# A four-layer graph network on one core: source of the one-hot comparison, place of the first head's edge weights, order of background steps, and place of the degree computation

## The chip, the cores and the metric

The kernel runs on one core of one Trainium2 chip. The metric is device microseconds of one execution; the time of a version is the median of its runs. The core has TensorE (PE, matrix products into PSUM), VectorE (DVE), ScalarE (ACT), GpSimd (POOL) and SyncE (SP, which issues all the DMAs here). Each engine works through its own queue in order, and semaphores make engines wait for each other.

## The reference

There are 512 nodes with 768 features and 16384 edges from `src` to `dst`. Four layers each add a graph part and a mixing part to x, and then a feed-forward part. The parts that the change touches are these:

```python
# layer 0: 8-headed attention over the edges, then one head on its result; layer 1 is of the same kind
e = leaky_relu(alpha_s[src] + alpha_d[dst], 0.2)
e = exp(e - segment_max(e, dst)[dst])
alpha = e / (segment_sum(e, dst)[dst] + 1e-16)
out = segment_sum(h[src] * alpha[:, :, None], dst)
# layers 2 and 3: degrees with self loops
deg = segment_sum(ones, col)                 # col = dst and one loop for each node
norm = rsqrt(deg)[row] * rsqrt(deg)[col]
out = segment_sum((x @ W)[row] * norm[:, None], col) + b
```

## The kernel before

The edges are turned once into a dense table `cnt` (512 x 512, rows are destinations, cut in four tiles of 128): how often each pair of nodes occurs. All attention over edges is then dense: for each destination tile, a row of source scores (`row_of`, L323 on: four transposes on PE of a score column spread over 128 columns) is added to `off`, which holds -1e30 where `cnt` is zero; the maximum, leaky ReLU and exponential follow, and the product with `cnt`, row sums and division give weights. `turned` (L770) transposes them by source, and `aggregate` multiplies them with h on PE.

**Counting.** `edge_counts` (L668) takes 128 steps of 128 edges, in five groups. Each step makes two one-hots, one of 512 for the source (L702 on DVE, or L699 and L700 on ACT in every second or third step) and one of 256 for the destination (L703 on DVE: node numbers `near` against the edge's destination, then times 1 or 4096, so that one product counts two halves of the destinations). Two matmuls (L706) accumulate the count. `nodes` lies in SBUF as fp16; `near` is its first half as fp32 in PSUM. After each group, ACT, DVE and POOL split the two halves and add them to `cnt` (L712 to L721). At the end `off` is made (L723, DVE) and `cnt` is stored.

**Products.** A 768-wide product is done as one level of Strassen: `strassen` makes 14 calls of `product` (L503), each with three matmuls in fp32 (two passes each in the profile), and sums their PSUM results on DVE (L541 to L562) with copies on ACT (L525). In order, one half of the output rows needs products 1 and 2 (the loaded weights alone), 3 to 5 (weight differences), the other half 6 to 10 in the same way, and then 11 to 14. The weight differences come from POOL (`SplitB`, L436 to L439, three times four operations), the activation's sums from `SplitA` (L418 to L421). `strassen_add` (L602) does the same for products that are added to x or h2.

**Background steps.** `tick()` runs one step of the first generator in the list `background`; `product` calls it after its matmuls. `pinned` sets what a step issues behind the last instruction before it on each engine; counting is exempt (`loose`) and gets seven steps a tick. `delayed(n, ...)` lets n ticks go by. `drain()` runs what is left. Within these ties a planner decides each engine's order ahead of time, by the order of the program and its own estimate of when data is ready.

**Layer 0.** 24 steps of counting run alone, 16 more after the first norm, and the rest inside head 0's products. The loop over `i` (L911) computes head i's h and its scores (`heads`; `node_scores`, L783, eight operations on DVE that multiply h by a row and sum), while the weights of head i-1 are turned as steps (delayed 8). Then it aggregates head i-1, makes head i's weights (`edge_weights`, L735), and projects head i-1 (`project`, `L0_gnn_W2`).

**Layer 1.** `cnt` is loaded again; POOL makes a positive `off` (L1346), PE and ACT transpose `cnt` to `cntT` (L1350, L1351), and DVE sums the degrees (L1352). Then comes the product with `gat_w1`, with the steps of `second_norm` (a norm of the rows of xn on DVE and ACT, and their transposes). `rest` (the second half of the first norm's transposes and the activation's sums) is called after the first four products. `heads1` and `last_edges` are background steps in the products that follow.

**Layers 2 and 3.** `gcn` uses `dinv`, made from the degrees at L1692 to L1699.

Of the kernel before, what the change touches and what calls it, by code (L numbers as in the profile page):

```python
# [97 lines left out]
def kernel(ctx: ExitStack, tc: tile.TileContext, a: dict, out: bass.AP):  # L98
# [103 lines left out]
    def evacuate(dst, src):  # L202
# [3 lines left out]
        else:  # L206
            V.tensor_copy(dst, src)

    epsc = const.tile([P, 2], FP, name="epsc")
    G.memset(epsc[:, 0:1], 1e-5)  # L210
# [285 lines left out]
    def strassen(A, B, use, feature, then=None, extra=None, fresh=False):  # L496
# [5 lines left out]

        def product(bank, a, b, c, start, stop):  # L503
            for k in range(KC // 2):
                if feature:
                    l, r = b[:, k, ts(c, P)], a[:, k, :]
                else:
                    l, r = a[:, k, ts(c, P)], b[:, k, :]
                T.matmul(bank, l, r, start=start and k == 0, stop=stop and k == KC // 2 - 1,  # L509
                         skip_group_check=True)  # L510
            tick()

# [78 lines left out]
    def strassen_add(A, B, add, then=None):  # L591
# [4 lines left out]

        def product(m, name, l, r, start):
            b = banks[m]
            if start:
                b[name] = psum()[:, :HC]  # L600
            for k in range(KC // 2):
                T.matmul(b[name], l[:, k, ts(m, P)], r[:, k, :], start=start and k == 0,  # L602
                         stop=k == KC // 2 - 1, skip_group_check=True)
            tick()
            return b[name]
# [62 lines left out]
    def edge_counts(gp):  # L668
# [24 lines left out]
        for g in range(n_groups):  # L693
            js = range(EC * g // n_groups, EC * (g + 1) // n_groups)
            acc = [psum() for _ in range(2)]
            for j in js:
# [4 lines left out]
                else:  # L701
                    V.tensor_scalar(oh[:, :N], nodes, ef[:, 0, j : j + 1], None, op0=ALU.is_equal)  # L702
                V.tensor_scalar(oh[:, N:], near, ef[:, 1, j : j + 1], far[:, j : j + 1],  # L703
                                op0=ALU.is_equal, op1=ALU.mult)
# [17 lines left out]
        for t in range(NT):  # L722
            V.tensor_scalar(off[:, t, :], cnt[:, t, :], 0.0, -BIG, op0=ALU.is_equal, op1=ALU.mult)  # L723
        nc.sync.dma_start(cnt_dram, cnt)
# [9 lines left out]

    def edge_weights(src4, dst4, gp, cnt, off):  # L735

        srow = row_of(src4)
        w = gp.tile([P, NT, N], FP, tag="edge_w", name="edge_w", bufs=1)
        mx = tiny(NT, name="ga_mx")
        for t in range(NT):  # L740
            V.tensor_tensor_reduce(w[:, t, :], srow, off[:, t, :], 1.0, -3.0e38,  # L741
                                   ALU.add, ALU.max, mx[:, t : t + 1])
        V.tensor_add(mx, mx, dst4)
        nm = tiny(NT, name="ga_nm")
        V.scalar_tensor_tensor(nm, mx, 0.2, mx, op0=ALU.mult, op1=ALU.max)
        V.tensor_scalar(nm, nm, -1.0, None, op0=ALU.mult)
        den = tiny(NT, name="ga_den")
        for t in range(NT):
            wt = w[:, t, :]
            S.activation(wt, wt, AF.Identity, bias=dst4[:, t : t + 1])  # L750
            V.scalar_tensor_tensor(wt, wt, 0.2, wt, op0=ALU.mult, op1=ALU.max)  # L751
            S.activation(wt, wt, AF.Exp, bias=nm[:, t : t + 1])
            V.scalar_tensor_tensor(wt, wt, 1.0, cnt[:, t, :], op0=ALU.mult, op1=ALU.mult,  # L753
                                   accum_out=den[:, t : t + 1])
        V.tensor_scalar(den, den, 1e-16, None, op0=ALU.add)
        V.reciprocal(den, den)
        for t in range(NT):
            V.tensor_scalar(w[:, t, :], w[:, t, :], den[:, t : t + 1], None, op0=ALU.mult)
        return w

# [118 lines left out]
    with tc.tile_pool(name="gat0", bufs=2) as gp:  # L879
# [16 lines left out]
        def project(i, sums):  # L896
# [11 lines left out]
            flush()  # L908

        done = None  # L910
        for i in range(9):  # L911
            if done:
                g, hg, ew = done
                wT = gp.tile([P, NT, N], FP, tag="edge_wT", name="edge_wT", bufs=wt_bufs[0])
                if i < 8:
                    background.append(delayed(8, turned(ew, wT)))
                else:
# [8 lines left out]
            if i < 8:  # L926
                done = i, h, edge_weights(s4, d4, gp, cnt, off)
            else:
                ys, va = performer_values(norm)
            if i:  # L930
                project(g, sums)
        x = load_x()
        qT = last_gat(h2, "g0_as", "g0_ad", gp, cnt, off, lambda: performer_features(ys, 0))
# [403 lines left out]
    cntT = late.tile([P, NT, N], FP, name="cntT")  # L1337
    deg = late.tile([P, NT], FP, name="deg")
    dinv = late.tile([P, NT], FP, name="dinv")
    HW = 96  # L1340
    with tc.tile_pool(name="gat1", bufs=1) as gp:
        off = gp.tile([P, NT, N], BF, name="off")
        cnt = token_major("cnt")[:, :, :N]
        nc.sync.dma_start(cnt, cnt_dram)
        for t in range(NT):
            G.tensor_scalar(off[:, t, :], cnt[:, t, :], 0.0, BIG, op0=ALU.is_equal, op1=ALU.mult)  # L1346
        for s in range(NT):
            ps = psum()
            for t in range(NT):
                T.transpose(ps[:, ts(t, P)], cnt[:, t, ts(s, P)], ident)  # L1350
            S.copy(cntT[:, s, :], ps)  # L1351
        V.tensor_reduce(deg, cnt, AX.X, ALU.add)  # L1352

# [28 lines left out]

        background.append(second_norm())

# [305 lines left out]
    for s in range(NT):  # L1690
        V.tensor_add(cntT[:, s, ts(s, P)], cntT[:, s, ts(s, P)], ident)
    V.tensor_scalar(deg, deg, 1.0, None, op0=ALU.add)  # L1692
    S.activation(dinv, deg, AF.Sqrt)
    V.reciprocal(dinv, dinv)
    nw = tiny(NT, name="ln_nw")
    V.tensor_mul(nw, dinv, dinv)
    V.tensor_mul(nw, nw, deg)
    V.tensor_scalar(nw, nw, -0.5, 1.5, op0=ALU.mult, op1=ALU.add)
    V.tensor_mul(dinv, dinv, nw)  # L1699

# [328 lines left out]
```

## Time and profile before

| | |
|---|---|
| median of 3 runs | 3117.9 us (3116.71 to 3118.49) |
| the profiled execution: its own time | 3118.86 us |
| its span, first to last instruction | 3117.1 us |
| mean granted TensorE clock | 0.987 |
| TensorE busy | 3014.7 us, 97% |
| VectorE busy | 1508.9 us, 48% |
| GpSimd busy | 1451.9 us, 47% |
| ScalarE busy | 745.8 us, 24% |
| chain that ended last | PE 85%, DVE 10%, ACT 2%, POOL 2% |

How to read it: the span is what the profile records; the execution's own time is 1.8 us more, and the profiled execution lies 1.0 us above the median. Times in the views are counted from the span's start. Busy time of an engine is summed over the span; a busy TensorE is not always at its peak, since the ends of pipelined matmuls are modelled. In the timeline each line has the start, the length, the engine, the source line, the operation, its output and input names with their shapes, the number of merged instructions, and in brackets how long the engine had stood idle and who released it. A length there includes some 0.09 us in which the next instruction on DVE has begun; the pitch from start to start is what one costs.

### The profile page before, as it was taken

How to read it: one execution, taken by the hardware profiler on the slowest of the kernel's cores; microseconds unless marked ns; L12 is line 12 of the kernel's file. 1: busy time of each engine (PE TensorE's matmuls, PEld its weight loads, DVE VectorE, ACT ScalarE, POOL GpSimd, SP SyncE). 2: the span in 40 equal slices, each digit the busy share in tenths (PEclk: the TensorE clock that was granted, in tenths of full speed). 3: DMA queues.
4: the chain of work that ended last, by engine and by line, in shares of the span. 5: the costliest groups of instructions: out<-in, count | busy, mean ns of one | idle time of the engine just before them, and what ended most of it. 6: DMA issues, size and time to landing. Idle time of an engine off the chain costs nothing.

```text
span 3117.1 us, 31594 instructions
## 1 busy us (share of the span) xinstructions
PE 3014.7 (97%) x11757; PEld 2006.2 (64%) x11757; DVE 1508.9 (48%) x3420; ACT 745.8 (24%) x1426; POOL 1451.9 (47%) x1535
## 2 busy tenths in 40 slices
PE   7799999999999999999989999999999999999989
PEld 3355555555766776765675357877777776677755
DVE  8954545455356235446766535433333335462241
ACT  7332222242253112103532212200000002221111
POOL 2544444443425563565552343555555558255610
PEclk9899999999999999999999999999999999999999
DMA  3121212221302222421111512122212223122222
GB/s 115 54 71 71 71 71 71 71 92 59 98 6 97 91 92 70 126 105 56 62 66 62 152 66 95 68 91 91 86 71 88 92 91 122 48 100 68 101 85 61
DMA packets 92691, 253.63 MB, mean 81 GB/s; under 512 B 9889, under 2 KB 14881, under 8 KB 91514
## 3 DMA queue, kind: packets, MB, share of 16 engines
q1 hardware_dynamic: 92538, 251.61, 23.3%
q8 instruction: 93, 1.52, 0.2%
q14 instruction: 60, 0.49, 0.1%
HBM read 244.23 MB, written 7.36 MB: 81 GB/s over the span
## 4 chain that ended last, share of the span: by engine, by line
PE 85%; DVE 10%; ACT 2%; POOL 2%; issue 1%; DMA 0%; SPq 0%; POOLq 0%; DVEq 0%; ACTq 0%
PE ps L509 41%; PE ps L602 23%; PE ps L888 5%; PE ps L306 4%; PE ps L1077 1%; DVE oh L703 1%; PE ps L1064 1%; PE ps L296 1%; PE ps L272 1%; PE ps L1910 1%; DVE edge_w L751 1%; PE ps L1565 1%; DVE edge_w L741 1%; DVE edge_w L753 1%; PE ps L1923 1%
## 5 line engine op out<-in xcount | busy, mean ns | idle before, releaser
L436 POOL TENSOR_TENSOR tw<-w 128x384 f32<-128x384 f32 x246 | 252.0, 1035 | 948.5 <-DMA w<-in_L_gnn_W 336.8
L509 PE MATMUL ps<-sx,w 128*128 128x256 f32 x1188 | 316.7, 380 | 3.6 <-DVE sx L418 2.8
L509 PE MATMUL ps<-sx,tw 128*128 128x256 f32 x1188 | 292.0, 382 | 4.2 <-DVE room L1434 3.2
L602 PE MATMUL ps<-w,sx 128*128 128x384 f32 x720 | 256.8, 486 | 4.4 <-DVE sx L418 3.1
L438 POOL TENSOR_TENSOR tw<-w 128x384 f32<-128x384 f32 x246 | 255.6, 1047 | 9.3
L439 POOL TENSOR_TENSOR tw<-w,tw 128x384 f32<-128x384 f32 x246 | 254.2, 1042 | 10.1
L437 POOL TENSOR_TENSOR w<-w 128x384 f32<-128x384 f32 x246 | 252.7, 1037 | 8.6
L509 PEld LDWEIGHTS ps<-sx,tw 128*128 128x128 f32 x1188 | 220.2, 190 | 47.7 <-DVE st_u L549 8.2
L602 PE MATMUL ps<-tw,sx 128*128 128x384 f32 x720 | 250.4, 487 | 0.0
L509 PEld LDWEIGHTS ps<-sx,w 128*128 128x128 f32 x1188 | 224.8, 190 | 39.3 <-PE ps L509 2.3
L525 ACT COPY st_p<-ps 128x256 f32<-128x256 f32 (+1 forms) x127 | 49.9, 394 | 719.7 <-PE ps L509 680.9
L549 DVE TENSOR_TENSOR st_u<-st_p,ps 128x256 f32<-128x256 f32 (+1 forms) x127 | 57.2, 450 | 337.3 <-PE ps L509 337.1
L602 PEld LDWEIGHTS ps<-tw,sx 128*128 128x128 f32 x720 | 136.1, 190 | 95.1 <-DVE x L1794 1.2
L602 PEld LDWEIGHTS ps<-w,sx 128*128 128x128 f32 x720 | 136.4, 190 | 94.5 <-POOL tw L439 4.3
L652 DVE TENSOR_TENSOR x<-x,ps 128x384 f32<-128x384 f32 x216 | 115.2, 552 | 165.7 <-PE ps L602 164.3
L509 PE MATMUL ps<-xfT,w 128*128 128x256 f32 x720 | 176.8, 380 | 0.2
L509 PE MATMUL ps<-w,sx 128*128 128x384 f32 x456 | 169.1, 490 | 2.4 <-DVE up_r L719 1.7
L888 PE MATMUL ps<-edge_wT,h 128*128 128x512 f32 x384 | 166.1, 592 | 0.0
L509 PE MATMUL ps<-tw,sx 128*128 128x384 f32 x456 | 162.2, 490 | 2.2 <-DVE st_u L549 2.1
L552 DVE TENSOR_TENSOR st_u<-st_p,ps 128x256 f32<-128x256 f32 (+1 forms) x127 | 57.2, 450 | 206.0 <-PE ps L509 206.0
L509 PEld LDWEIGHTS ps<-xfT,w 128*128 128x128 f32 x720 | 135.9, 190 | 24.1 <-issue 1.3
L602 PE MATMUL ps<-w,hid 128*128 128x384 f32 x432 | 142.9, 488 | 0.0
(482 smaller groups left out, 5111.0 us busy)
## 6 DMA issues: line engine op xcount, KB each, us to landing
w<-in_L_gnn_W SPq DMA_DIRECT2D x60, 768.0 KB, 6.4
w<-in_L_mix_fc_w SPq DMA_DIRECT2D x48, 768.0 KB, 6.4
row<-in_rows SPq DMA_DIRECT2D x39, 384.0 KB, 4.4
w<-in_L_mix_qkv_w SPq DMA_DIRECT2D x18, 768.0 KB, 5.2
w<-in_L_ffn_w SPq DMA_DIRECT2D x18, 768.0 KB, 7.1
w<-in_L_ffn_routed_gate SPq DMA_DIRECT2D x18, 768.0 KB, 5.9
w<-in_L_ffn_routed_up SPq DMA_DIRECT2D x18, 768.0 KB, 6.8
w<-in_L_ffn_routed_down SPq DMA_DIRECT2D x18, 768.0 KB, 5.7
```

The lines of the kernel that those rows point to most:

```text
L306: T.matmul(ps, parts[k][:, ts(t, P)], w_of(k)[:, ts(c, HC)], start=k == 0, stop=k == n - 1)
L436: G.tensor_sub(tt[:, 0, k], b22[:, k], b12[:, k])
L437: G.tensor_sub(b12[:, k], b12[:, k], b11[:, k])
L438: G.tensor_sub(tt[:, 1, k], b22[:, k], b12[:, k])
L439: G.tensor_sub(tt[:, 2, k], b21[:, k], tt[:, 1, k])
L509: T.matmul(bank, l, r, start=start and k == 0, stop=stop and k == KC // 2 - 1, skip_group_check=True)
L525: S.copy(b["p1"], b["x"])
L549: V.tensor_add(b["u2"], b["p1r"], b["y"])
L552: V.tensor_add(u3, b["p1r"], b["y"])
L602: T.matmul(b[name], l[:, k, ts(m, P)], r[:, k, :], start=start and k == 0, stop=k == KC // 2 - 1, skip_group_check=True)
L652: V.tensor_add(x[:, t, ts(j, HC)], x[:, t, ts(j, HC)], ps)
L888: T.matmul(ps, h[:, s, ts(f, P)], wT[:, s, :], start=s == 0, stop=s == NT - 1)
```

## The change

1. `edge_counts`: from step 32 (the 33rd) on, L703 compares `nodes[:, :HT]` (fp16, SBUF) in place of `near` (fp32, PSUM).
2. `off` in layer 0 is made by four ACT operations, Relu(1e30 - 1e30 cnt), in place of four on DVE; it is positive now, and L741 subtracts it.
3. `edge_weights` becomes a generator `weighing` that stops after `row_of`, after the maxima, and after each second tile. Head 0 doesn't make its weights after its own products: in head 1 they are background steps after five idle ticks, and the turning follows with no idle ticks. Other heads call it in one piece as before.
4. Both `product` functions call `tick()` ahead of their matmuls.
5. `deg` and `dinv` are computed from `cnt` in layer 0, written after head 1's projection (`degrees`), with a constant tile for `dinv`; the code at L1352 and L1692 to L1699 goes.
6. Layer 1: `second_norm` gets three idle ticks; the transposes of `cnt` and `off` (now on ACT) become the steps of `by_sources` behind it.

```diff
+    bigc = const.tile([P, 1], FP, name="bigc")
+    G.memset(bigc, BIG)
...
         def product(bank, a, b, c, start, stop):
+            tick()
             for k in range(KC // 2):
...
-            tick()
...
         def product(m, name, l, r, start):
+            tick()
             b = banks[m]
...
-            tick()
             return b[name]
...
-                V.tensor_scalar(oh[:, N:], near, ef[:, 1, j : j + 1], far[:, j : j + 1],
+                V.tensor_scalar(oh[:, N:], near if j < 32 else nodes[:, :HT], ef[:, 1, j : j + 1], far[:, j : j + 1],
                                 op0=ALU.is_equal, op1=ALU.mult)
...
         for t in range(NT):
-            V.tensor_scalar(off[:, t, :], cnt[:, t, :], 0.0, -BIG, op0=ALU.is_equal, op1=ALU.mult)
+            S.activation(off[:, t, :], cnt[:, t, :], AF.Relu, bias=bigc, scale=-BIG)
...
-    def edge_weights(src4, dst4, gp, cnt, off):
+    def weighing(w, src4, dst4, cnt, off):
 
         srow = row_of(src4)
-        w = gp.tile([P, NT, N], FP, tag="edge_w", name="edge_w", bufs=1)
+        yield
         mx = tiny(NT, name="ga_mx")
         for t in range(NT):
             V.tensor_tensor_reduce(w[:, t, :], srow, off[:, t, :], 1.0, -3.0e38,
-                                   ALU.add, ALU.max, mx[:, t : t + 1])
+                                   ALU.subtract, ALU.max, mx[:, t : t + 1])
...
+        yield
         den = tiny(NT, name="ga_den")
...
+            if t % 2:
+                yield
...
+    def edge_weights(src4, dst4, gp, cnt, off):
+        w = weight_tile(gp)
+        for _ in weighing(w, src4, dst4, cnt, off):
+            pass
         return w
...
+        dinv = const.tile([P, NT], FP, name="dinv")
+
+        def degrees():
+            deg = tiny(NT, name="deg")
+            V.tensor_reduce(deg, cnt, AX.X, ALU.add)
+            V.tensor_scalar(deg, deg, 1.0, None, op0=ALU.add)
+            S.activation(dinv, deg, AF.Sqrt)
+            V.reciprocal(dinv, dinv)
...
                 if i < 8:
-                    background.append(delayed(8, turned(ew, wT)))
+                    if i == 1:
+                        background.append(delayed(5, weighing(ew, s4, d4, cnt, off)))
+                    background.append(delayed(0 if i == 1 else 8, turned(ew, wT)))
...
-                done = i, h, edge_weights(s4, d4, gp, cnt, off)
+                done = i, h, edge_weights(s4, d4, gp, cnt, off) if i else weight_tile(gp)
...
+            if i == 2:
+                degrees()
...
-        for t in range(NT):
-            G.tensor_scalar(off[:, t, :], cnt[:, t, :], 0.0, BIG, op0=ALU.is_equal, op1=ALU.mult)
-        for s in range(NT):
-            ps = psum()
-            for t in range(NT):
-                T.transpose(ps[:, ts(t, P)], cnt[:, t, ts(s, P)], ident)
-            S.copy(cntT[:, s, :], ps)
-        V.tensor_reduce(deg, cnt, AX.X, ALU.add)
+
+        def by_sources():
+            for s in range(NT):
+                ps = psum()
+                for t in range(NT):
+                    T.transpose(ps[:, ts(t, P)], cnt[:, t, ts(s, P)], ident)
+                S.copy(cntT[:, s, :], ps)
+                S.activation(off[:, s, :], cnt[:, s, :], AF.Relu, bias=bigc, scale=-BIG)
+                yield
...
-        background.append(second_norm())
+        background.append(delayed(3, second_norm()))
+        background.append(by_sources())
...
-    V.tensor_scalar(deg, deg, 1.0, None, op0=ALU.add)
-    S.activation(dinv, deg, AF.Sqrt)
-    V.reciprocal(dinv, dinv)
```

## The prediction

> **What bounds the kernel now.** The page comes first: engine totals.
>
> ```profile
> PE 3014.7 (97%) x11757; PEld 2006.2 (64%) x11757; DVE 1508.9 (48%) x3420; ACT 745.8 (24%) x1426; POOL 1451.9 (47%) x1535
> ```
>
> TensorE (PE) is the bound of nearly the whole span; only stretches where it stands idle or runs below its pace can give time back. The change touches three. I cut the span there with the view of busy time by stretch.
>
> ```profile
> core 0: us, PE busy (x) PEld busy (x) DVE busy (x) ACT busy (x) POOL busy (x), PEclk, DMA share, GB/s
> 39.50:119.90 80.40, 72.16 (x283) 32.34 (x281) 77.39 (x184) 44.10 (x74) 15.50 (x12) 1.00 0.00 1
> 119.90:172.10 52.20, 36.48 (x106) 19.57 (x106) 46.85 (x70) 13.62 (x25) 38.14 (x28) 0.80 0.26 82
> 172.10:250.99 78.89, 77.69 (x238) 42.66 (x237) 37.50 (x78) 23.92 (x42) 34.94 (x36) 1.00 0.20 70
> ...
> 1416.27:1440.00 23.73, 16.83 (x63) 10.32 (x62) 15.59 (x34) 9.32 (x20) 16.70 (x15) 0.86 0.10 42
> ```
>
> Row 1 is edge counting from about step 33 on beside head 0's products: VectorE (DVE) is full. Row 2 runs from head 0's last product to head 0's aggregation. Row 3, one later head, shows PE full: nothing to win there. Row 4 is the start of layer 1. What PE does at full clock, from matmul pitches in the timeline (0.215 us for L706, 0.323 for a 384-wide L509 pass, 0.108 for a transpose): row 1 has 193 L706 + 78 L509 + 12 transposes = 41.5 + 25.2 + 1.3 = 68.0, so 12.4 us are lost; row 2 has 84 L509 + 20 transposes = 29.3, so 22.9 are lost. Next, PE's waits in the first 200 us (total us, times, longest), and its timeline (start, us; in brackets idle before and who ended it).
>
> ```profile
> PE ps L706 <- DVE oh L703: 14.9, 7, 10.0
> PE ps L327 <- DVE st_u L783: 12.4, 4, 10.2
> ```
> ```profile
> 130.10 0.48 PE L327 MATMUL ps<-ident,ga_sc 128*128 128x128 f32 x1 [10.18 <-DVE st_u L783]
> ...
> 158.51 0.33 PE L774 MATMUL ps<-ident,edge_w 128*128 128x128 f32 x1 [0.35 <-DVE edge_w L758]
> ...
> 1425.90 5.97 PE L509 MATMUL ps<-w,xnT 128*128 128x384 f32 x12 [5.59 <-ACT st_p L525]
> ```
>
> 10.0 of the 14.9 us precede the first one-hot and stay. The 10.18 us is row_of's first transpose at the head of PE's queue, with head 1's products, whose first two need only loaded weights, behind it.
>
> **Node numbers from SBUF (96 steps).**
>
> ```profile
> 52.66 1.35 DVE L702 TENSOR_SCALAR oh<-nodes,ef 128x512 bf16<-128x512 f16 x1
> ...
> 54.98 0.34 DVE L702 TENSOR_SCALAR oh<-nodes,ef 128x512 bf16<-128x512 f16 x1
> 55.24 0.99 DVE L703 TENSOR_SCALAR oh<-ps,ef,far 128x256 bf16<-128x256 f32 x2
> ```
>
> L703 has a pitch of 0.45 us. No row has two pointers on fp16 in SBUF. Nearest is L702: 512 columns, one pointer, pitch 0.26. Half the columns save about 0.07; the second pointer adds at most 0.13 (two-pointer L280 is 0.457 where the plain copy L207 of the same PSUM shape is 0.33). That gives 0.19 to 0.27; the other bound is no gain, 0.47 (256 columns at the 1.04 ns of the 768-wide L420, plus pointers). I take 0.27, nearest the row: 96 x 0.18 = 17 us off DVE, whose 77.4 fall to 60, below PE's 68.0. PE becomes the bound. Against this speaks the Trainium skill, SBUF — State Buffer, "SBUF: two separate sides": a VectorE operation in a two-port mode and a GpSimd operation lock each other out for a whole instruction. The 1.35 us row, beside a POOL add, shows it for L702. Taken for every new L703 beside the 16 adds of 1.3 us, the rule would cost up to 16 us and eat the 17. But only as many waits can occur as adds, and L702 and L717 already suffer one or so per group (1.0, 0.4, 1.1, 0.5 us): I count no more than 4 us extra, inside DVE's new 8 us of slack. Of the 12.4 lost I leave 3.4 for group ends (PE's pauses of 1.4, 0.8, 0.9 us around L719): **gain 9.0**, bounds -2 and 12.4. Head 0 then ends at T = 119.9 - 9.0 = 110.9.
>
> **Head 0's weights as steps in head 1, `off` on ACT.** The four L723 (1.2, 1.2, 0.4, 1.2 us) leave DVE; four ACT operations of about 0.6 us (like L700's 0.63) come, beside an ACT 26% busy in row 2: free, or 2.4 us if it were the last. Subtracting a positive `off` in L741 is the same operation (0.61), and bigc's memset (0.1 us) falls in POOL's idle time before 11.5 us. srow's transposes stand before product 6, so PE no longer waits 10 us. What is late next is POOL, which makes head 1's weight differences while locked with node_scores:
>
> ```profile
> 127.10 2.12 POOL L436 TENSOR_TENSOR tw<-w 128x384 f32<-128x384 f32 x2
> ...
> 142.53 1.98 POOL L437 TENSOR_TENSOR w<-w 128x384 f32<-128x384 f32 x2
> ...
> 159.39 1.05 POOL L439 TENSOR_TENSOR tw<-w,tw 128x384 f32<-128x384 f32 x1
> ```
>
> It starts 7.2 us after counting's last matmul; with ticks ahead, counting ends two products (3.9 us) before T, so at T+3.4. Product 3 needs the L437 that ended 17.4 us after the start: T+20.8. Products 1, 2, 6, 7 fill PE's first 7.8 us; 3 to 5 end at T+26.6. Scores (3 us of leftovers + 8 x 1.67) are done by T+17. The weights' maxima are pinned behind product 5's sum, T+26.6. Before, the weights took 141.65 to 160.65 less 1.5 of other work = 17.5 us, locked with POOL; head 1's own took 193.18 to 202.98 plus scaling = 11.3, unlocked. POOL is busy to T+36.7: 10.1 us cover 58% of the work, 42% of 11.3 = 4.8 follow, plus 1.5 for chunk 1's sums: T+43. The other seven products end at T+40.2. With 1.2 for the first transposes and copy, aggregation starts at T+44.2, against 52.2 before: **gain 8.0**, bounds -1.7 (first rival) and 21.7 (PE's 29.3 plus 1.2).
>
> **Steps ahead of products elsewhere.** Each step moves one product (1.3 to 1.9 us) earlier; spacing, hence the chain behind each, stays. turned, the routers, heads1 and last_edges have row 3's kind of slack: 0, bounds -3 and +3. SP's row loads in those steps move with them, ahead of weight loads issued tens of us before use.
>
> **Degrees.** The planner hoists work whose data is ready:
>
> ```profile
> 2.94 0.17 DVE L1240 TENSOR_SCALAR qb<-cols 128x6 f32<-128x6 f32 x1
> ```
>
> So the reduction may land right after the counts, where DVE waits from T+17 to T+26.6: 2.3 us plus tiny operations (up to 0.9 each beside POOL), and a Sqrt that can cost two 1.28 us table loads. Hidden in that gap; uncovered, up to 5.5 + 2.6. I take **-0.5**. The four dinv operations at 1775.4 to 1778.8 leave no PE wait: 0.
>
> **Layer 1.**
>
> ```profile
> 1417.06 2.29 DVE L1352 TENSOR_REDUCE deg<-cnt 128x4 f32<-128x2048 f32 x1 [0.19 <-issue]
> ...
> 1420.19 2.13 DVE L1692 TENSOR_SCALAR deg<-deg 128x4 f32<-128x4 f32 x1
> ```
> ```profile
> 1424.46 1.03 ACT L252 ACTIVATE xn<-xn,ln_nb,ln_rs 128x768 f32<-128x768 f32 x1 [1.23 <-DVE ln_nb L251]
> 1425.39 0.84 ACT L525 COPY st_p<-ps 128x384 f32<-128x384 f32 x2
> ```
>
> The copies that products 3 and 4 of PE's queue need sit on ACT behind the second norm, which sits behind deg on DVE. With deg gone, norm steps three products later and cntT after them, the copies run at about 1418.3. PE: four products to 1424.0, rest's transposes 1.3, their copies 1.1, early's two 3.9, so first sums at 1430.3 against 1439.97. Of these 9.7, 1.3 (y's transposes) and 1.7 (cntT's) are moved, not saved: **gain 6.5**, bounds 2 and 8. `off`'s 7.9 us leave POOL, idle there anyway; ACT gains 4 x 0.6 beside the last products. cnt holds its buffer some 25 us longer; xnT's comes free first, so I cost that at 0 (up to 2).
>
> **Sum.** 9.0 + 8.0 - 0.5 + 6.5 = 23.0. Span 3117.1 - 23.0 = 3094.1; that execution took 3118.9, 1.8 outside the span: 3095.9; the median 3117.9 is 1.0 below it: **3095**.
>
> **Rivals.**
> - Queue order in head 1 (0.14): the transposes of ew stand ahead of products 11 to 14. For: at 158.51 the planner put them so, and PE waited. Against: by unlocked times it will find the weights late. Then aggregation is at T+43 + 9.6 + 1.3 = T+54: head 1 gives -1.7, sum 13.3: 3105.
> - L703 keeps its pace (0.09): first gain 0, sum 14: 3104. That is the change not doing what it says.
> - POOL releases early (0.09): products 3 on start ten us sooner, aggregation near T+34, counting at its floor: 9 + 3 + 18 + 6.5 - 0.5 = 36: 3082.
> - Slower (0.08): the same wedge, with degrees' 5.5 and table loads' 2.6 us in front of the weights, and PE's clock halved after the wait (in 130 to 140 the granted clock was 0.50, a pass 0.69 us). Products 11 to 14 then take 15.5; aggregation is at weights + 18.5. With counting's 9.0 and layer 1's 6.5 kept, the total turns slower from weights at T+49 (49 + 18.5 against 52.2 + 15.5); at T+51 it gives 3120, at T+55 3124.
> - Forecast (0.60): 3087 to 3103.
>
> A measurement of this kernel tells about 0.2% (6.2 us) from no change. Faster is forecast, queue order, pace and early POOL: 0.92. Of the slower case 0.06 lies within 0.2%, 0.02 beyond. The range 3084 to 3109 takes in the rivals at 3104 and 3105; it leaves out the early-POOL case and the slower one, 0.17.
>
> **What would show it.** L703 after step 32 at a pitch near 0.27; row 1's work ending near 111 us with DVE no longer full; L327 without a 10 us wait; the first L888 near 155; a lone wait of products 3 for POOL's L437; no st_p wait near 1420 and the first sums product about 9 us after the fourth. Wrong: L774 early in PE's queue with a long wait, L703 at 0.45, or deg between the weights.

## The result and the profile after

The changed kernel takes 3098.89 us (median of 4 runs, 3097.94 to 3099.33) where the kernel before takes 3117.31 (4 runs, 3113.12 to 3118.49): a ratio of 0.9943, 95% interval 0.9926 to 0.996, so faster by 0.57%. The forecast was 3095, range 3084 to 3109. The profiled execution took 3099.04 us, its span is 3097.2, 19.9 less than before; the forecast for the span was 23.0 less.

The engine totals of the changed kernel, and its busy time by stretch (its two rows answer to rows 1 and 2 of the prediction's view; in brackets the count of instructions):

```profile
PE 3005.4 (97%) x11757; PEld 2006.2 (65%) x11757; DVE 1482.7 (48%) x3416; ACT 749.7 (24%) x1434; POOL 1436.3 (46%) x1532
```
```profile
core 0: us, PE busy (x) PEld busy (x) DVE busy (x) ACT busy (x) POOL busy (x), PEclk, DMA share, GB/s
40.80:111.20 70.40, 67.33 (x269) 34.10 (x268) 62.87 (x178) 43.34 (x74) 18.20 (x14) 0.98 0.00 1
111.20:156.30 45.10, 34.31 (x105) 19.45 (x104) 37.42 (x68) 14.80 (x26) 31.52 (x27) 0.89 0.31 107
```

Counting beside head 0 takes 70.4 us in place of 80.4, and DVE (62.9 busy) is no longer full; PE is the fuller engine, as forecast. The timeline of DVE there shows the one-hots' pitch, 0.25 to 0.26 us for L705 (L703 before) and for L704 (L702 before):

```profile
85.01 0.34 DVE L704 TENSOR_SCALAR oh<-nodes,ef 128x512 bf16<-128x512 f16 x1
85.28 0.33 DVE L705 TENSOR_SCALAR oh<-nodes,ef,far 128x256 bf16<-128x256 f16 x1
85.53 0.34 DVE L704 TENSOR_SCALAR oh<-nodes,ef 128x512 bf16<-128x512 f16 x1
```

PE's waits in the first 200 us (total, times, longest): the wait for node_scores ahead of row_of (12.4 us) is gone, and a wait for GpSimd's weight differences (L439; L437 before) of 10.1 us has come. PE's timeline in head 1 shows where:

```profile
PE ps L708 <- DVE oh L705: 13.9, 4, 11.3
PE ps L512 <- POOL w L439: 10.1, 2, 6.7
```
```profile
128.41 1.65 PE L512 MATMUL ps<-w,sx 128*128 128x384 f32 x2 [6.72 <-POOL w L439]
129.86 3.85 PE L512 MATMUL ps<-tw,sx 128*128 128x384 f32 x6
...
136.39 0.60 PE L329 MATMUL ps<-ident,ga_sc 128*128 128x128 f32 x4
...
156.30 1.88 PE L901 MATMUL ps<-edge_wT,h 128*128 128x512 f32 x4
```

The six matmuls at 129.86 take 3.85 us where six at 134.35 take 2.20: after the wait PE runs at a lower clock (0.50 from 126.6 to 133.4 us, 0.89 over the stretch). row_of's transposes then start without a wait, and the aggregation starts at 156.30, against 171.94.

**The path cut in four.** A is first one-hot matmul to aggregation (counting and head 1), C is from the start of layer 0's last product to the first kv,qT product of layer 1's linear attention, D is all that follows. What lies between A and C is 1236.9 to 1237.6 us in every kernel here, and the first one-hot matmul comes at 10.0 us before, 11.3 after and 10.3 to 11.2 in the others: A, C and D don't contain that accident. Times in us.

| kernel | median | ratio to before (95%) | span | A | C | D |
|---|---|---|---|---|---|---|
| before | 3117.3 | | 3117.1 | 161.9 | 203.4 | 1504.4 |
| changed | 3098.9 | 0.9943 (0.9926 to 0.996) | 3097.2 | 145.0 | 199.2 | 1504.7 |
| e1 one-hot from PSUM | 3112.2 | 0.9972 (0.9961 to 0.9983) | 3109.8 | 158.3 | 199.2 | 1504.8 |
| e2 weights whole | 3105.9 | 0.9951 (0.9938 to 0.9965) | 3106.2 | 151.8 | 201.1 | 1505.2 |
| e3 steps behind | 3092.4 | 0.9908 (0.9895 to 0.9922) | 3091.5 | 148.0 | 194.5 | 1500.5 |
| e4 degrees late | 3101.7 | 0.9937 (0.9924 to 0.9949) | 3101.6 | 144.2 | 201.1 | 1508.1 |
| e9 ahead in heads 0, 1 only | 3089.5 | 0.9915 (0.9902 to 0.9929) | 3090.8 | 144.1 | 194.8 | 1504.1 |
| e10 one tick later | 3101.5 | 0.9951 (0.9938 to 0.9965) | 3100.8 | 144.5 | 203.8 | 1504.9 |
| e11 e9, split free | 3084.8 | 0.9897 (0.9884 to 0.9911) | 3083.8 | 139.3 | 195.9 | 1500.5 |
| e12 e9, nodes in all steps | 3096.5 | 0.9933 (0.9921 to 0.9945) | 3094.5 | 148.7 | 194.7 | 1503.6 |
| e13 step before split | 3099.8 | 0.9949 (0.9937 to 0.9962) | 3098.0 | 144.5 | 201.1 | 1504.9 |
| e14 e11, layer 1 as before | 3091.2 | 0.9925 (0.9913 to 0.9938) | 3089.0 | 138.9 | 198.7 | 1503.7 |
| e15 e3, split free | 3086.3 | 0.9906 (0.9892 to 0.992) | 3087.2 | 142.2 | 195.8 | 1500.5 |
| e16 e11, norm at once | 3088.7 | 0.9913 (0.9899 to 0.9927) | 3086.7 | 139.5 | 195.7 | 1503.5 |

e1 to e4, e9 to e12 and e13 to e16 each shared one chip with runs of before, at 3121.05, 3116.51 and 3116.24 us. A ratio's interval is about 4 us to each side, the changed kernel's 5. The four kernels with equal code in A (changed, e9, e10, e13) have 144.1 to 145.0 us there, so less than 0.9 decides nothing in A. In C and D equal code agrees only to the 2 to 3 us of the granted clock (last section). There a second split helps: the time in which PE stood idle (the stretch less PE's busy time), and the busy time lost to a lower clock (half of what PE was busy while the traces' clock records say 0.50). The first is read from these rows, C of before, of the changed kernel and of e3:

```profile
1409.35:1612.73 203.38, 182.52 (x920) 134.99 (x919) 141.50 (x347) 90.10 (x169) 109.25 (x95) 0.95 0.15 58
1393.27:1592.45 199.18, 179.71 (x920) 132.08 (x919) 135.93 (x344) 93.02 (x172) 101.26 (x91) 0.98 0.16 57
1396.48:1590.97 194.49, 180.60 (x920) 133.62 (x918) 132.15 (x344) 92.57 (x172) 100.64 (x91) 0.96 0.17 60
```

PE is idle for 20.9, 19.5 and 13.9 us of C, and loses 7.6, 3.2 and 5.5 us to the clock. In A the two stand in for each other: in the four kernels with equal code 17.8 to 21.5 us are idle and 7.2 to 3.0 lost to the clock, and the sum is 24.5 to 25.3.

### The profile page after: what moved, and what is told of

Read it like the earlier page. It is cut to its first block, busy times and chain, and to the rows that moved or that the text cites. A ratio compares the mean times of both kernels' runs of the same rounds, so it can differ in the third digit from the quotient of the medians.

```text
span 3097.2 us, 31606 instructions
## 1 busy us (share of the span) xinstructions
PE 3005.4 (97%) x11757; PEld 2006.2 (65%) x11757; DVE 1482.7 (48%) x3416; ACT 749.7 (24%) x1434; POOL 1436.3 (46%) x1532
## 3 DMA queue, kind: packets, MB, share of 16 engines
q8 instruction: 93, 1.52, 0.2%
## 4 chain that ended last, share of the span: by engine, by line
PE 86%; DVE 8%; POOL 2%; ACT 2%; issue 1%; DMA 0%; SPq 0%; POOLq 0%; ACTq 0%
PE ps L512 43%; PE ps L605 23%; PE ps L901 5%; PE ps L308 4%; PE ps L1109 1%; PE ps L1096 1%; PE ps L298 1%; PE ps L274 1%; PE ps L1934 1%; PE ps L1597 1%; POOL room L1455 1%; DVE edge_w L754 1%; DVE edge_w L743 1%; PE ps L1947 1%; PE ps L1324 1%
## 5 line engine op out<-in xcount | busy, mean ns | idle before, releaser
L439 POOL TENSOR_TENSOR w<-w 128x384 f32<-128x384 f32 x246 | 252.7, 1036 | 8.8
L441 POOL TENSOR_TENSOR tw<-w,tw 128x384 f32<-128x384 f32 x246 | 251.7, 1030 | 10.3
L551 DVE TENSOR_TENSOR st_u<-st_p,ps 128x256 f32<-128x256 f32 (+1 forms) x127 | 57.1, 450 | 346.7 <-PE ps L512 346.6
L512 PE MATMUL ps<-w,sx 128*128 128x384 f32 x456 | 170.3, 494 | 11.9 <-POOL w L439 10.1
L554 DVE TENSOR_TENSOR st_u<-st_p,ps 128x256 f32<-128x256 f32 (+1 forms) x127 | 57.1, 449 | 200.8 <-PE ps L512 200.8
```

Source lines behind the costliest of these rows:

```text
L439: G.tensor_sub(b12[:, k], b12[:, k], b11[:, k])
L441: G.tensor_sub(tt[:, 2, k], b21[:, k], tt[:, 1, k])
L551: V.tensor_add(b["u2"], b["p1r"], b["y"])
L554: V.tensor_add(u3, b["p1r"], b["y"])
```

## The experiments

**e1, e2, e3, e4: one part of the change undone each.** e1 takes the node numbers of L705 from PSUM again:

```diff
-V.tensor_scalar(oh[:, N:], near if j < 32 else nodes[:, :HT], ...
+V.tensor_scalar(oh[:, N:], near, ...
```

> The changed kernel, but L705 compares the PSUM copy of the node numbers in all 128 steps. Theory A (VectorE's pace of 0.45 us a step bounded the counting): head 0's last product ends near 119 us again instead of 111.2, everything after it as in the changed kernel, so 3107 to 3108 us. Theory B (the 8.7 us come from counting standing ahead of the products): head 0 ends at 111 to 113, 3099 to 3101 us.

Head 0's last product ends at 118.9, so theory A holds: counting was bound by VectorE. A grows by 13.3 us and the span by 12.6, more than either theory allowed. Counted from the first one-hot, 8.4 of the 13.3 lie ahead of head 0's end; the other 4.9 lie in head 1, where PE now waits 5.0 us for a copy of ScalarE (st_p). By the ratios the whole is 0.29%, 9 us.

e2 makes head 0's weights in one piece again, after head 0's products:

```diff
-if i == 1:
-    background.append(delayed(5, weighing(ew, s4, d4, cnt, off)))
-background.append(delayed(0 if i == 1 else 8, turned(ew, wT)))
+background.append(delayed(8, turned(ew, wT)))
...
-done = i, h, edge_weights(s4, d4, gp, cnt, off) if i else weight_tile(gp)
+done = i, h, edge_weights(s4, d4, gp, cnt, off)
```

> The changed kernel, but head 0's edge weights are made in one piece ahead of head 1's products, as before, and turned after eight idle ticks. Theory A (the first transposes at the head of TensorE's queue cost the wait): TensorE waits 8 us or more for scores, aggregation starts about 7 us later after head 0's end (52 against 45.1), 3106 us. Theory B (GpSimd's differences of head 1's weights bound the stretch in either order): aggregation at 45 to 47 us after head 0's end, 3099 to 3101 us.

A grows by 6.8 us, 6.2 of them idle time of PE. The aggregation starts 52.2 us after head 0's end, as theory A had it, and the wait for node_scores is back in PE's waits of the first 200 us:

```profile
PE ps L329 <- DVE st_u L796: 9.8, 4, 6.2
```

C differs by 1.9 us, of which 1.7 lie where the code is the same and the granted clock was 0.96 in place of 1.00. By the ratios the whole is 2.5 us with an interval wider than that, so the size is read from A.

e3 puts `tick()` behind the matmuls again in both `product` functions:

```diff
         def product(bank, a, b, c, start, stop):
-            tick()
             for k in range(KC // 2):
...
+            tick()
...
```

> The changed kernel, but each step stands behind its product again. Theory A (the order only sets when counting ends against head 0's last product, and with it when GpSimd may start on head 1's weights): counting ends with head 0, GpSimd starts some 4 us later, aggregation about 4 us later, 3102 to 3104 us. Theory B (the order is free): 3098 to 3100 us. In layer 1 both expect less than 1.5 us of difference.

This is faster than the change: 0.9908 against 0.9943, 5.7 us by the spans. A is 3.0 us longer, near theory A's 4, but C is 4.7 shorter and D 4.2, where both theories had allowed less than 1.5. In C it is PE's waits that fell (13.9 us of idle time against 19.5), not the clock. In D, 2.4 us are `last_edges` (31.2 us from its first product to L1597's in place of 33.6) and 1.1 a stretch whose granted clock was higher. The prediction had put all of this at 0.

e4 computes the degrees in layer 1 again, the reduction after the load of `cnt` and the rest ahead of layer 2:

```diff
-            if i == 2:
-                degrees()
...
         nc.sync.dma_start(cnt, cnt_dram)
+        V.tensor_reduce(deg, cnt, AX.X, ALU.add)
...
```

> The changed kernel, but the degrees are summed in layer 1 from the reloaded counts, and the rest of their code stands before the graph convolutions, as before. Theory A (with the second norm three products later, the reduction on VectorE blocks nothing that TensorE waits for; in layer 0 the degree operations stood in front of the weights' maxima for about 0.8 us): 3098 to 3100 us. Theory B (the degree operations were what made TensorE wait 5.6 us at the start of layer 1): a wait of 4 to 5 us for the st_p copies returns, 3102 to 3104 us.

By the ratios there is no difference. A is 0.8 us shorter, but that lies ahead of the last one-hot matmul, where the code is the same: from its end to the aggregation it is 48.8 us both with the degrees and without. C is 1.9 longer and D 3.4, mostly by the clock (2.2 and 2.6 us more lost to it); PE's idle time in C is 19.2 us against 19.5, and the wait for st_p did not return, so theory B fell, and theory A's time was missed by less than the clock took. What the degrees did in the changed kernel shows in DVE's timeline: the reduction ran right after counting, and their small operations, 3.0 us in all, stood ahead of L554 and the weights' maxima (L743). L554's product ended near 136.5, so L554 was some 0.7 us late, but nothing of this reached the aggregation:

```profile
113.86 2.29 DVE L928 TENSOR_REDUCE deg<-cnt 128x4 f32<-128x2048 f32 x1 [1.77 <-POOL cnt L723]
...
136.49 0.84 DVE L936 TENSOR_TENSOR dinv<-dinv,ln_nw 128x4 f32<-128x4 f32 x1
137.25 0.54 DVE L554 TENSOR_TENSOR st_u<-st_p,ps 128x384 f32<-128x384 f32 x1
...
138.30 0.68 DVE L743 CUSTOM_DVE_ANT_0 edge_w<-ps,off 128x512 f32<-128x512 f32 x1
```

**Where steps ahead of products cost.** PE's waits for the exponentials in heads1 (L1464 for L1457) between 1440 and 1600 us are 5.4 us in before, 11.3 in the changed kernel, 5.6 in e3. The longest in the changed kernel, 5.36 us, in the timeline of all engines:

```profile
1547.31 0.99 POOL L441 TENSOR_TENSOR tw<-w,tw 128x384 f32<-128x384 f32 x1
1548.26 2.49 POOL L1455 TENSOR_TENSOR room<-room 128x512 f32<-128x512 f32 x2
1549.55 0.72 ACT L1457 ACTIVATE room<-room,ed_b 128x512 f32<-128x512 f32 x1 [6.31 <-POOL room L1455]
...
1550.33 0.90 PE L1464 MATMUL ps<-ident,room 128*128 128x128 f32 x3 [5.36 <-ACT room L1457]
```

The L441 is the last of twelve SplitB operations (1536.16 to 1548.30) that GpSimd worked through ahead of the two subtractions the step needed. In e3 the planner put the same subtractions between the SplitB operations, and PE waited 1.17 us here and 1.52 for the second one, 2.7 us less than the changed kernel:

```profile
1545.10 1.25 POOL L1455 TENSOR_TENSOR room<-room 128x512 f32<-128x512 f32 x1
1546.32 0.99 POOL L439 TENSOR_TENSOR w<-w 128x384 f32<-128x384 f32 x1
1546.38 0.72 ACT L1457 ACTIVATE room<-room,ed_b 128x512 f32<-128x512 f32 x1 [6.87 <-POOL room L1455]
...
1547.16 0.66 PE L1464 MATMUL ps<-ident,room 128*128 128x128 f32 x4 [1.17 <-ACT room L1457]
```

Two kernels ask why. e10 leaves the steps ahead but starts them one tick later:

```diff
-background.append(heads1())
+background.append(delayed(1, heads1()))
...
-background.append(last_edges())
+background.append(delayed(1, last_edges()))
```

> The changed kernel with one idle tick in front of heads1 and one in front of last_edges: each step there stands again where it stood against the products before the change, but still behind the DVE and ACT work that follows the product ahead of it. Theory A (the cost of steps ahead is that a step is tied behind the sums and copies of the preceding product, so its own chain starts after them): nothing comes back, within 1.5 us of the changed kernel, PE's waits for the exponentials (L1464) at 10 us or more. Rival B (the cost is that a step comes one product too early, before the engine that feeds it is done): heads1's 2.6 and last_edges' 2.3 us come back, 4.9 in all, and the L1464 waits fall to some 6 us.

Nothing comes back in heads1: C is 203.8 (22.9 us of PE's idle time against 19.5, and 2.1 more lost to the clock), and the L1464 waits are 14.8 us; the longest, 6.4, again follows two subtractions right behind the last of twelve SplitB operations. Only last_edges gets 1.3 us shorter. So it isn't that a step comes one product too early. e13 issues a step ahead of the SplitB instead of between it and the first product:

```diff
         def __init__(self, w):
+            if early_tick:
+                tick()
+                ticked.append(1)
...
+    early_tick, ticked = [], []
+
+    def ahead_of_product():
+        if ticked:
+            ticked.pop()
+        else:
+            tick()
...
-            tick()
+            ahead_of_product()
...
         background.append(heads1())
+        early_tick.append(1)
```

> The changed kernel (steps ahead of products everywhere), but from heads1 on the step that would stand between a weight's differences (SplitB) and the first product after them is issued before those differences. The place of every step against the sums is left as the change has it. Theory A (the cost of steps ahead in heads1 and last_edges is that a step's GpSimd subtractions are tied behind twelve operations of SplitB that happen to stand between): PE's waits for the exponentials (L1464) fall from 12.8 to 7 us or less, and 2.5 to 4.9 us come back: ratio near 0.993 where the changed kernel has 0.9943. Rival B (the cost is the place behind the sums and copies of the product before): nothing comes back, within 1.5 us of the changed kernel, L1464 waits still at 10 us or more.

Theory A fell in the form it was put: the waits are 11.2 us and no time comes back (ratio 0.9949). But the trace also shows that the twelve operations still ran ahead of the same subtractions (1536.71 to 1548.84). Outside head 1, SplitB isn't tied to anything, so the planner may move it past steps that were issued earlier. What is shown is that in the kernels with steps ahead (changed, e13) these subtractions end up behind the twelve operations, and with steps behind (e3) they don't. That the step's ACT work, tied behind the copies of the product before, makes the planner think them late would explain e10 and e13, but that is argued, not shown.

e9 keeps steps ahead in heads 0 and 1 alone (a list `ahead`, emptied at i == 2, says which of two places calls `tick`):

```diff
+            if ahead:
+                tick()
             for k in range(KC // 2):
...
+            if not ahead:
+                tick()
...
+            if i == 2:
+                ahead.clear()
```

> The changed kernel with the steps ahead of the products only in heads 0 and 1 of layer 0, and behind them in all that follows. Theory A (the order was worth 3 us in head 1 and cost some 11 us in the later stretches; the two don't touch each other): head 1 as in the changed kernel (145 us from the first one-hot's matmul to the aggregation, where e3 had 148.0), the later stretches as in e3 (43.6, 150.9 and 1500.5 us), so 3 us less than e3, 0.990 of the kernel before, faster than every kernel so far. Rival B (the planner's later order hangs on where head 1 leaves the engines, so that the gains don't add): e3's 0.991 or slower, with the later stretches between e3's and the changed kernel's.

By stages theory A held: A is 144.1 and C 194.8, as in the changed kernel and in e3. The total did not follow: 0.9915 against e3's 0.9908, the same within the intervals. D is 3.6 us longer than e3's, 2.0 of it from the first kv,qT product to the next stage (granted clock 0.92 against 0.96) and 1.5 around the last head (0.95 against 0.97), in the same code. The 3.9 us won in A were there, and 3.5 of them were lost to the clock in D.

**What holds head 1.** e11 is e9 with the weight differences of head 1 untied:

```diff
-B = pinned(lambda: SplitB(w1)) if i == 1 else SplitB(w1)
+B = SplitB(w1)
```

> e9 with the weight differences of head 1 no longer tied behind the work before them, so that GpSimd may make them while edges are still counted. Theory A (GpSimd, late with L439, is what holds head 1 after the change, by 10.1 us of waits): those waits go, the weights start earlier, the aggregation comes 4 to 6 us earlier, minus 1 to 2 us for locked one-hots in counting: 3 to 4 us faster than e9. Rival B (the lock between VectorE and GpSimd is only moved: VectorE's one-hots wait for the 12 operations instead of the scores and weights): no faster than e9, 0 to 4 us slower, with the last one-hot's matmul later than 109 us.

GpSimd makes them at 25.1 to 37.9 us, right after head 0's. A shrinks by 4.8 us against e9, the ratio from 0.9915 to 0.9897: GpSimd was what bound head 1; the clock doesn't explain it (5.1 us lost to it in A, more than e9's 3.0). The last one-hot matmul ends at 107.93 instead of 106.05, so up to 1.9 us were paid in counting. PE's largest new wait in the first 170 us is now for VectorE:

```profile
PE ps L514 <- DVE st_u L555: 5.8, 2, 5.3
```

This version is faster than the change as well as the kernel before, by 0.5% and 1.0%. e15 is the same with steps behind products everywhere (e3 with the untied differences):

> Steps behind products everywhere, as in e3, with head 1's weight differences free, as in e11. Theory A (the order of steps in head 1 was worth 3 to 4 us only while GpSimd was late; with its differences made early the order is worth little, and e9's later stretches gave the rest back): within 1.5 us of e11. Rival B (the order in head 1 is worth the same with or without GpSimd's lateness): 3 us slower than e11, the aggregation 3 us later.

A is 2.9 us longer than e11's, C and D are equal, the total 1.5 (medians) to 3.4 us (spans) longer: rival B. (Here the 2.9 are all clock: 14.7 us idle in both, 7.9 against 5.1 lost to it.) The order in head 1 is worth its 3 us with or without GpSimd's lateness.

**Node numbers from SBUF in all steps.** e12 is e9 with `nodes[:, :HT]` in place of `near` for j < 32 too:

```diff
-near if j < 32 else nodes[:, :HT]
+nodes[:, :HT]
```

> e9 with the node numbers from SBUF in all 128 steps, so also in the first 32, of which 24 run with nothing else on PE and while GpSimd splits head 0's weights (12 operations from 11 to 25 us). Theory A (locks cost only as many waits as GpSimd has operations, and VectorE is the bound there): 32 x 0.18 = 5.8 us less on VectorE, minus up to 2.5 for locks: 3 us faster than e9. Rival B (the Trainium skill's rule in full: in the first steps VectorE and GpSimd shut each other out, an operation at a time): the gain is eaten, e9's time or up to 4 us more, GpSimd's split ends later than 27 us.

It is 4.6 us slower in A, 7.0 by the medians: rival B in kind, beyond its bound of 4, but GpSimd's split is not late (it ends at 24.96, e9's at 25.26). VectorE pays: its first 24 steps end at 27.62 in place of 24.23. The timeline of e12 and, below it, of e9 at the same place (GpSimd's and VectorE's lines):

```profile
14.98 1.12 POOL L441 TENSOR_TENSOR tw<-w,tw 128x384 f32<-128x384 f32 x1
...
15.17 1.97 DVE L712 TENSOR_SCALAR oh<-nodes,ef,far 128x256 bf16<-128x256 f16 x2
...
16.07 0.99 POOL L438 TENSOR_TENSOR tw<-w 128x384 f32<-128x384 f32 x1
```
```profile
14.93 1.09 POOL L441 TENSOR_TENSOR tw<-w,tw 128x384 f32<-128x384 f32 x1
15.08 0.98 DVE L712 TENSOR_SCALAR oh<-ps,ef,far 128x256 bf16<-128x256 f32 x2
```

Two SBUF one-hots take 1.97 us, one per GpSimd operation; two from PSUM take 0.98 beside the same operations. In the 13.4 us of the split e12 made 13 of them, 1.02 us each in the median, and e9 made 21 at 0.53. Here the rule of the Trainium skill (SBUF — State Buffer, "SBUF: two separate sides": an operation in a two-port mode and one of GpSimd shut each other out for a whole instruction) is seen one operation at a time. How the 3.4 us become 4.6 is not shown: PE's idle time in A is the same in both (21.7 and 21.5 us), and 4.0 us more are lost to the clock (it was 0.50 from 35.5 to 42.3 us, among others, where e9 had it full). The rule did not decide the change itself, since GpSimd is busy for only 18 of the 70 us after step 32.

**Layer 1.** Both kernels here are built on e11. e16 only takes the three idle ticks from `second_norm`:

```diff
-background.append(delayed(3, second_norm()))
+background.append(second_norm())
```

e14 does this too, and makes `off` on GpSimd and the transposes of `cnt` ahead of the product, as before the change; the degrees stay in layer 0:

```diff
-S.activation(off[:, s, :], cnt[:, s, :], AF.Relu, bias=bigc, scale=-BIG)
...
-background.append(by_sources())
...
+for t in range(NT):
+    G.tensor_scalar(off[:, t, :], cnt[:, t, :], 0.0, BIG, op0=ALU.is_equal, op1=ALU.mult)
+for _ in by_sources():
+    pass
```

> e11 (steps behind products from head 2 on, free weight differences in head 1) with layer 1 started as before the change: second_norm without idle ticks, off on GpSimd and the transposes of cnt ahead of the product with gat_w1; the degrees stay in layer 0. Theory A (layer 1's rearrangement is worth 8.9 us by itself and lost half of it only by the steps ahead): 7 to 9 us slower than e11, with a wait for st_p of 4 us or more. Rival B (most of that came from taking the degrees out of VectorE's queue, which this kernel keeps): 1 to 4 us slower than e11.

> e11 with second_norm started without its three idle ticks. Theory A (the ticks let the copies of products 3 and 4 run ahead of the norm on ScalarE; that is most of layer 1's gain): a wait for st_p of 2 us or more comes back near 1415, 2 to 5 us slower than e11. Rival B (the degrees' absence alone frees the copies, and a norm three products earlier takes away VectorE's late sums L551/L555): same or up to 3 us faster.

PE's waits for st_p in C, none in e11, are these in e14 and, below it, in e16:

```profile
PE ps L514 <- ACT st_p L531: 4.1, 2, 2.5
PE ps L514 <- ACT st_p L531: 2.1, 2, 1.6
```

e14 is slower than e11 by 0.28%, 8.7 us by the ratios and 5.2 by the spans. The wait is theory A's, but of the 5.2 only 2.8 are in C, which is rival B's size; the rest is a lower clock in the last 150 us. e16 is slower than e11 by 3.9 (medians) or 2.9 (spans), but its C is 0.2 us shorter, and 2.7 of the spans' difference are the same lower clock. Its waits for st_p came back, and rival B's saving of as much stood against them. So the three ticks are worth nothing in layer 1's own time where the degrees are gone. e4 shows the other side: with the ticks in place, the degrees in layer 1 bring no wait for st_p. No run takes back both. Moving `off` and the transposes of `cnt` is best read from e14 against e16, which differ in that alone: C is 3.0 us longer in e14, by PE's idle time (16.8 against 13.9 us), with 7.0 and 6.8 us lost to the clock.

## Why the prediction was right, and where it was not

The forecast of 3095 was 3.9 us too low. Counting and head 1 came as reasoned; one step of the argument (steps ahead of products elsewhere) failed, and the total stayed close with some luck, told under layer 1. In the span, 19.9 came of 23.0: 16.9 in A (forecast 16.5), 0.4 between A and C, 4.2 in C (6.5), -0.3 in D (0), and -1.3 because the profiled execution's first one-hot came 1.3 us later than before.

- **Node numbers, forecast gain 9.0.** Right in kind and size: the pitch of L705 is 0.26 where 0.27 was taken, the last product of head 0 ends at 111.2 where 110.9 was forecast, PE is the bound. A gain of 8.7, or 10.0 counted from the first one-hot; undone in e1, 8.4 counted so. Locks in the 70 us stayed small: two of the 96 new one-hots took over 0.6 us. That they would not have in the first 32 steps is e12.
- **Head 0's weights as steps, forecast gain 8.0.** Right: 6.9 in place, 6.8 undone (e2). GpSimd was the late one, as the forecast named it, and the working came stage by stage: GpSimd began at T+2.6 (forecast T+3.4), the weights' maxima at T+27.1 (T+26.6), the weights were done at T+41.9 (T+43), aggregation came at T+45.1 (T+44.2). The release of products 3 to 5 came in two waits, 3.4 and 6.7 us, in place of one, with a lower clock behind each. (GpSimd's start in before, 7.2 us in the forecast, was counted from head 0's end; behind the last one-hot matmul it was 7.8.) That GpSimd bound it was confirmed by e11, which is most of what the rival "POOL releases early" asked for, and gave 4.8 us, not 10: VectorE's scores and sums became late next.
- **Steps ahead of products elsewhere, forecast 0, bounds -3 and +3.** This step failed. "spacing, hence the chain behind each, stays" held against the products, but not against other instructions: the steps' subtractions on GpSimd got behind a weight's twelve differences. The cost is 4.4 to 4.7 us in C and 2.4 in last_edges (e3, e9), some 7 us, and the gain of steps ahead in head 1, 3 to 4 us, had been counted under head 1. By the spans the whole part, that gain included, costs 5.7 us.
- **Degrees, forecast -0.5.** Nothing that can be told (e4): 48.8 us from the last one-hot matmul to the aggregation with them and without. The reduction hid in DVE's gap as forecast, and so, in the end, did the small operations, though they made L554 0.7 us late. The four dinv operations before layer 2 cost nothing that can be told from the clock.
- **Layer 1, forecast gain 6.5, bounds 2 and 8.** (9.7 less the forecast's own 1.3 and 1.7 is 6.7, not 6.5.) The first half was right: no st_p wait, and the first sums product came 19.5 us after the last product of layer 0 (forecast 20.9, before 30.6). What is late next was missed. Inside the same product VectorE queued the sum L551 behind the norm's transposed copies (L282) and sums (L422, L420), in the timeline of all engines:

```profile
1428.59 1.45 DVE L282 TENSOR_SCALAR yT<-ps,cols 128x256 f32<-128x256 f32 x3 [2.36 <-ACT yT L285]
...
1431.69 0.55 DVE L551 TENSOR_TENSOR st_u<-st_p,ps 128x384 f32<-128x384 f32 x1
...
1432.29 0.59 PE L512 MATMUL ps<-tw,sx 128*128 128x384 f32 x1 [3.26 <-DVE st_u L551]
```

That and three waits of 1.1, 0.8 and 0.7 us took 5.9 back, and heads1's waits 5.9 more. So PE's idle time in C fell by 1.4 us only (20.9 to 19.5). That C is 4.2 us shorter all the same is in part luck: 4.4 us less were lost to the clock (7.6 to 3.2), which the forecast had not counted. Of these, 1.9 lie right behind the wait that went (the clock was 0.50 from 1422.8 to 1429.6 us in before), the rest elsewhere.

With steps behind products, PE's idle time in C is 13.9 to 15.4 us (e3, e9, e11, e15), 5.5 to 7.0 less than before, and C is 7.5 to 8.9 shorter: the size was about right for the part alone, and the order of the steps took most of it. Of those 5.5 to 7.0, `off` and the transposes of `cnt` are worth 2.9 (e14 against e16). The rest stays open between the degrees and the three ticks: each alone brings no loss when undone (e4, e16), and e14, with 4.1 us less idle time in C than before, differs from before in its layer 0 as well.

Of the rivals, "queue order" and "keeps pace" did not occur: L787 came when the weights were there, and L705 has its pitch. The slower case's lower clock occurred, but for 3.4 and 6.8 us, where before had 20.5 in a row.

## What to carry to other kernels

A background step moved by one place keeps its distance to the products, not to what else is queued on the engines that feed it; look at each engine's queue at the new place, above all where a dozen operations of another job stand, and measure each stretch, since one order may be right in one stage and wrong in the next. When a wait is removed, work out who releases the same product second (here GpSimd, then VectorE): it caps the gain. Here the one-hot from SBUF was faster for VectorE than the one from PSUM (0.26 against 0.45 us) only where GpSimd was mostly quiet; beside GpSimd's back-to-back operations it was slower (1.97 against 0.98 us for two).

## What the hardware showed beyond that

Kernels with the same instructions in a stretch took up to 3 us different times there, by the granted clock. D of e11 and of e16 is the clearest case: 1500.5 and 1503.5 us, with PE idle for 29.2 and 29.5, and 8.3 and 11.0 us lost to the clock. In the last 150 us there is a stretch of some 15 us in which PE is partly idle and its clock falls to 0.50. The busy time by stretch of 5 us in e11 (first) and e16 (PE's order is the same there; the clock is the third number from the end):

```profile
2988.80:2993.80 5.00, 2.21 (x11) 2.24 (x11) 2.48 (x8) 0.00 (x0) 0.00 (x0) 0.68 0.00 0
2993.80:2998.80 5.00, 3.43 (x16) 3.35 (x16) 2.55 (x13) 0.00 (x0) 0.00 (x0) 0.50 0.00 0
2998.80:3003.80 5.00, 5.00 (x10) 2.00 (x9) 3.08 (x6) 0.46 (x1) 0.00 (x0) 0.79 0.01 3
```
```profile
2981.70:2986.70 5.00, 4.25 (x21) 2.88 (x24) 1.52 (x6) 2.05 (x5) 0.00 (x0) 0.73 0.28 68
2986.70:2991.70 5.00, 2.32 (x14) 0.97 (x8) 1.54 (x8) 2.09 (x3) 0.00 (x0) 0.84 0.00 0
2991.70:2996.70 5.00, 3.02 (x15) 3.05 (x15) 1.70 (x5) 0.00 (x0) 0.00 (x0) 0.50 0.01 3
2996.70:3001.70 5.00, 3.44 (x13) 2.85 (x14) 3.37 (x14) 0.00 (x0) 0.00 (x0) 0.50 0.00 0
3001.70:3006.70 5.00, 5.00 (x9) 1.99 (x9) 2.27 (x4) 0.52 (x1) 0.00 (x0) 0.72 0.00 0
```

Taking the clock as either 1 or 0.5, e11 spent 2 x (0.32 + 0.50 + 0.21) x 5 = 10.3 us at half, and e16 2 x (0.27 + 0.16 + 0.50 + 0.50 + 0.28) x 5 = 17.1: three and five times some 3.4. The clock records in the traces say the same: 10.24 us from 2990.6 in e11, 3.41 from 2984.0 and 13.65 from 2990.8 in e16. In all fourteen traces they hold no other share than 1 and 0.50, and every stretch at 0.50 that ends inside the span lasts 3.41 us or 2, 3, 4 or 6 times that. This fits the Trainium skill (TensorE: Matmul & The Clock Gate, "Part 1: The HAM clock gate"), by which the gate looks at activity in windows of some 3.4 us that run free of the kernel. The same idle stretch would then cover one or two windows more or fewer, as its place falls, and 2.7 us of e16's end would need no edit of its own. No run here moved such a stretch on purpose to test it.
